# An attention kernel's PSUM banks: from a fixed rotation to a queue in which the sixth transposition bank behind a score piece is the first one's

## The chip, the cores and the metric

The kernel runs on one core of one Trainium2 chip, in float32 throughout. The time is the device time of one launch in microseconds (us); the kernel before has a median of 2784.84 us over three runs (2784.79 to 2785.24). A profile of one further execution shows what each engine did: TensorE (PE in the views, with its weight loads apart as PEld), VectorE (DVE), ScalarE (ACT), GpSimd (POOL) and SyncE (SP), which issues the DMAs.

## The reference, cut to what matters

An encoder layer over a short context (2 x 77 tokens) and a decoder layer over 2 x 2048 tokens, of width 512 with 16 heads of 32. The part that the change touches is the decoder's causal self-attention with a bias by relative distance:

```python
q, k, v = ...                                   # 16 heads of 32, each 2048 tokens, two batches
scores = jnp.einsum('bhqd,bhkd->bhqk', q, k) / jnp.sqrt(hd)
scores = scores + bias[None]                    # by distance; -inf above the diagonal
attn = jax.nn.softmax(scores, axis=-1)
out = jnp.einsum('bhqk,bhkd->bhqd', attn, v)
```

After it come the cross-attention to the 77 encoded tokens and a feed-forward of width 2048.

## The kernel before, in words

**Units.** The self-attention is cut into 128 units (b, m, g, t): batch b, block m of 512 queries (0 to 3), group g of four heads (0 to 3), tile t of 128 queries (0 to 3). A unit has n = 4m + t + 1 key tiles of 128 keys. `pieces` (L315) cuts them into pieces of up to four: n = 6 gives 4 + 2, n = 13 gives 4 + 4 + 3 + 2.

**Scores.** `scores` (L357) takes a piece: four banks of PSUM, one for each head of the group; one matmul for each head (L374; the four heads use four row groups of the array and run side by side). VectorE then empties the four banks in the order of the heads, with L383 for key tiles far from the diagonal and L390 for the last two, which get the bias; in a unit's last piece a head can need both. After the last piece comes the maximum of maxima (L399, tile `nm`), and four exponentials on ScalarE (L404) are put in a list, from which `exps` issues one or two at a time at fixed places.

**Turns.** `turn` (L410) transposes the probabilities of up to two pieces of a unit, so with m above 0 up to eight key tiles. For each key tile, called a load here, it takes one bank, makes four transpositions into it (L424, one for each head) and has the bank copied to SBUF: by ScalarE (L430) for the first half of the loads, by VectorE (L428) for the second. Behind the fourth load it issues one exponential, behind the last another. `values` (L435) then multiplies the copies with the value rows (L441) into bank 7.

**Order.** All engines take their instructions in program order. The loop at L1730 goes through the turns: the scores of a piece further on are issued as soon as their probabilities' place is free, which in nearly all cases is right ahead of a turn; then the turn; then, at a unit's end, a `slot` of other work (projections at L215 and L1018, normalisations at L305, cross-attention, all with banks of their own); more scores; an exponential or two; the values.

**Banks.** Of the eight banks of PSUM, bank 7 belongs to `values`. The other seven go round: `bank()` (L179) hands out 0, 1, ... 6, 0, ... to whoever asks. Scores take four in a row, a turn one for each load. An instruction that writes into a bank waits until the bank's last reader is done. After the attention, `count` is set so that only banks 0 to 3 go round, and the feed-forward uses 4 to 7 by an order of its own.

**Which bank is whose.** Call the seven banks just behind a score piece a, b, c (the oldest) and s0 to s3 (the piece's heads). With the rotation the loads of the turn that follows take a, b, c, s0, s1, s2, s3, a. The eighth load meets the first load's bank again, and loads four to seven write into the banks that VectorE empties of the scores.

Transpositions with m = 0 are cut in another way (`first`, four loads for each piece) and have no more than four loads in a turn.

Of the kernel before, what the change touches and what calls it, by code (L numbers as in the profile page):

```python
# [22 lines left out]
HC = P // HD  # L23
# [31 lines left out]
def tile_encoder_decoder(ctx: ExitStack, tc: tile.TileContext, ins, out):  # L55
# [103 lines left out]
    with (  # L159
# [14 lines left out]
        oT_all = ac.tile([P, 6, TB * P], F32, name="oT")  # L174
        bo = ac.tile([P, D], F32, name="row_dec_sa_out_b")
        psum = ps.tile([P, 8, 512], F32, name="psum")
        count = {"bank": 0, "banks": 7, "pts": 0, "oT": 0, "mm": 0}

        def bank():  # L179

            i = count["bank"] % count["banks"]
            count["bank"] += 1
            return psum[:, i, :]

        def in_turn(what, tile):
            i = count[what] % tile.shape[1]
            count[what] += 1
            return tile[:, i, :]

        def rows4(r):  # L190
            return slice(r * HD, (r + 1) * HD)
# [19 lines left out]
        def q_job(b, m, g):  # L211
            def run(w):
                mm = bank()
                for c in range(NC):
                    nc.tensor.matmul(mm, w[:, c, :], nTs[b, m][:, c, :], start=(c == 0), stop=(c == NC - 1))  # L215
                q = sb.tile([P, MB], F32, name="q", tag="q", bufs=3)
                nc.vector.tensor_scalar(q, mm, vec("dec_sa_in_b", g), SCALE, ALU.add, ALU.mult)
                qTs[b, m, g] = q

            return lambda: small_w(g * P), run, True  # L220

        def k_job(b, m, g):
            def run(w):
                mm = bank()
                for c in range(NC):
                    nc.tensor.matmul(mm, w[:, c, :], nTs[b, m][:, c, :], start=(c == 0), stop=(c == NC - 1))
                d, bi = kT[:, g, ts(m, MB)], vec("dec_sa_in_b", NC + g)
                if m >= 2:
                    nc.vector.tensor_scalar(d, mm, bi, None, ALU.add)
                else:  # L230
                    nc.scalar.activation(d, mm, AF.Identity, bias=bi)

            return lambda: small_w(D + g * P), run, True

        def v_job(b, m, t):
            def run(w):
                mm = bank()
                for c in range(NC):
                    nc.tensor.matmul(
                        mm, nTs[b, m][:, c, ts(t, P)], w[:, c, :], start=(c == 0), stop=(c == NC - 1)  # L240
                    )
                nc.vector.tensor_copy(vv[:, m * TB + t, :], mm)

            return lambda: big_w("v"), run, False
# [99 lines left out]
        def probabilities(n):  # L344
            w = (units[n][1] + 1) * MB
            at = END - HC * w if n % 2 else 0
            p = pp[:, at : at + HC * w].rearrange("p (k r x) -> p r k x", r=HC, x=P)
            return [p[:, r] for r in range(HC)]
# [3 lines left out]
        def exps(k):  # L352

            for _ in range(min(k, len(late_exps))):
                late_exps.pop(0)[1]()

        def scores(n, k0, kn):  # L357
            b, m, g, t = units[n]
            i = m * TB + t
            if k0 == 0:  # L360
                state[n] = {
                    "p": probabilities(n),
                    "mx": sm.tile([P, HC, 8], F32, name="mx", tag="mx"),
                    "nm": sm.tile([P, HC], F32, name="nm", tag="nm"),
                    "col": 0,
                }
                if t == 0:
                    sums_of[b, m, g] = sm.tile([P, TB, HC], F32, name="sums", tag="sums")
            st = state[n]
            last = k0 + kn == i + 1  # L370
            q = qTs[b, m, g]
            banks = [bank() for _ in range(HC)]
            for r in range(HC):
                nc.tensor.matmul(  # L374
                    banks[r][:, : kn * P], q[rows4(r), ts(t, P)], kT[rows4(r), g, k0 * P : (k0 + kn) * P],
                    start=True, stop=True,
                )
            far = max(0, kn - 2) if last else kn
            col = st["col"]
            for r in range(HC):  # L380
                p, s, c = st["p"][r], banks[r].rearrange("p (k x) -> p k x", x=P), col
                if far:
                    nc.vector.tensor_scalar(  # L383
                        p[:, k0 : k0 + far], s[:, :far], 1.0, None, ALU.mult, ALU.max,
                        accum_out=st["mx"][:, r, c : c + 1],
                    )
                    c += 1
                if last:
                    near = biases[b, m, g][:, r, :].rearrange("p (k x) -> p k x", x=P)
                    nc.vector.tensor_tensor_reduce(  # L390
                        p[:, k0 + far : i + 1], s[:, far:kn], near[:, 2 - (kn - far) :], 1.0, LOWEST, ALU.add, ALU.max,
                        accum_out=st["mx"][:, r, c : c + 1],
                    )
                    c += 1
            st["col"] = c
            if not last:
                return

            nc.vector.tensor_reduce(st["nm"], st["mx"][:, :, :c], AX.X, ALU.max, negate=True)  # L399
            for r in range(HC):  # L400
                p, nm, to = st["p"][r][:, : i + 1], st["nm"][:, r : r + 1], sums_of[b, m, g][:, t, r : r + 1]

                def run(p=p, nm=nm, to=to):
                    nc.scalar.activation(p, p, AF.Exp, bias=nm, accum_out=to)  # L404

                late_exps.append((n, run))
# [3 lines left out]
        def turn(pieces):  # L410

            first = units[pieces[0][0]][1] == 0
            loads = []
            for n, k0, kn in pieces:
                ks = range(k0, k0 + kn)
                if first:
                    loads += [[(n, k, r) for k in ks] for r in range(HC)]
                else:
                    loads += [[(n, k, r) for r in range(HC)] for k in ks]
            for o, load in enumerate(loads):  # L420
                pt = bank()
                pts = in_turn("pts", pts_all).rearrange("p (x q) -> p x q", q=P)
                for x, (n, k, r) in enumerate(load):
                    nc.tensor.transpose(pt[:, ts(x, P)], state[n]["p"][r][:, k], ident)  # L424
                    got[n, k, r] = pts[:, x, :]
                w = len(load) * P
                if o % 2 if first else o >= (len(loads) + 1) // 2:
                    nc.vector.tensor_copy(pts[:, : len(load), :], pt[:, :w])  # L428
                else:
                    nc.scalar.copy(pts[:, : len(load), :], pt[:, :w])  # L430
                if not first and o == min(3, len(loads) - 1):
                    exps(1)
            exps(HC if first else 1)
# [634 lines left out]
        for x, (b, m) in enumerate(blocks):  # L1068
            u = x * NU
            first = m == 0  # L1070
# [11 lines left out]
            else:  # L1082
# [8 lines left out]
                for at, names in todo.items():  # L1091
                    for name in names.split():
                        i = int(name[1])
# [140 lines left out]
        def late_loads():  # L1234
            nc.vector.tensor_scalar(qbias, vecs[:, _COL["dec_ca_in_b"] : _COL["dec_ca_in_b"] + NC], SCALE, None, ALU.mult)
            for t in range(TB):
                new_y(1, t)
            nc.sync.dma_start(kTc, ckT_d[:, :, :S])
            for _ in range(2):
                t = sb.tile([P, HC, 2 * P], F32, name="bias", tag="bias", bufs=2)  # L1240
                qT.append(t.rearrange("p (g a) k -> p g (a k)", g=2))
# [478 lines left out]
        def score_next():  # L1720
            n, k0, kn = stream[at[0]]
            scores(n, k0, kn)
            scored_to[n] = k0 + kn
            at[0] += 1
# [4 lines left out]
        i = 0  # L1729
# [28 lines left out]
        for t in (2, 3):  # L1758
            residual_load(*blocks[-1], t, pts_all[:, 2 * t - 3, :])
        late_loads()  # L1760
        count.update(bank=0, banks=4)
        side = cross(1)
        slot(end)
        for s in range(4):
# [58 lines left out]
```

## Time and profile before

| what | us |
|---|---|
| median of three runs | 2784.84 |
| lowest, highest | 2784.79, 2785.24 |
| the profiled execution's own time | 2785.57 |
| its span in the profile | 2783.8 |
| self-attention: last transposition starts at | 1706.9 |

The profile's page gives each engine's busy time over the span, and groups of instructions by line. The views used below are: the page; the timeline, which lists instructions of one engine in order of time and joins those that follow each other without idle time (start, duration, engine, line, operation, output <- inputs, shape, count, and in brackets the idle time before with what ended it); the waits, which sum idle time by line and by what ended it; and windows, which give busy time of every engine within stretches of the span. A row of weight loads (PEld) is the better witness for TensorE's progress here than a row of matmuls, since a matmul's row reaches over the next one's start: a weight load starts when its instruction may start. In timeline rows times are rounded to 0.01 us.

### The profile page before, as it was taken

What the parts mean: (1) busy time and instruction counts of PE and PEld (TensorE: products, weight loads), DVE (VectorE), ACT (ScalarE), POOL (GpSimd) and SP (SyncE); (2) the same over time, 40 slices, a digit from 0 to 9 for tenths busy, and PEclk for the clock granted to TensorE, in tenths of its full rate; (3) what the DMA queues carried; (4) which work ended last, traced back from release to release, by engine and by line L of the source; (5) the groups of instructions that cost most, each with busy time, mean ns of one, the idle gap of its engine ahead of it and who ended that gap; (6) DMA issues with size and microseconds to landing.
All of it is one profiled execution on the core that took longest, in us unless ns stands there. A gap on an engine that the chain in (4) does not pass through costs nothing. (4 is left out here: it accounts for less than half of the span.)

```text
span 2783.8 us, 66824 instructions
## 1 busy us (share of the span) xinstructions
PE 2757.1 (99%) x26294; PEld 2137.0 (77%) x26294; DVE 1885.9 (68%) x5412; ACT 1439.6 (52%) x2761; POOL 915.2 (33%) x777
## 2 busy tenths in 40 slices
PE   9999999999999999999999999999999999999998
PEld 5577776677666566676677667898989898989898
DVE  5676587788887578687788895555555646464645
ACT  3544455656666556666656665434444444444431
POOL 1501134400100412212300002364646474746456
PEclk9999999999999999999999999999999999999999
DMA  7423345421112521233211004574748575656475
GB/s 224 140 88 110 111 129 161 128 59 38 38 55 58 142 76 55 89 100 103 96 55 40 25 32 138 182 236 155 230 155 233 179 224 162 221 163 222 147 227 182
DMA packets 282252, 362.45 MB, mean 130 GB/s; under 512 B 39073, under 2 KB 156625, under 8 KB 281811
## 3 DMA queue, kind: packets, MB, share of 16 engines
q1 hardware_dynamic: 281938, 358.18, 42.0%
q8 instruction: 208, 3.41, 0.5%
q14 instruction: 106, 0.86, 0.1%
HBM read 314.49 MB, written 43.59 MB: 129 GB/s over the span
## 5 line engine op out<-in xcount | busy, mean ns | idle before, releaser
L404 ACT ACTIVATE pp<-pp,nm 128x128 f32<-128x128 f32 (+15 forms) x512 | 612.1, 1202 | 143.8 <-DVE nm L399 139.3
L383 DVE TENSOR_SCALAR_CACHE_REDUCE pp<-psum 128x512 f32<-128x512 f32 (+3 forms) x1024 | 558.9, 591 | 59.1 <-PE psum L374 57.4
L424 PEld LDWEIGHTS psum<-ident,pp 128*128 128x128 f32 x4352 | 475.8, 142 | 110.0 <-DVE pp L383 56.0
L430 ACT COPY pts<-psum 128x512 f32<-128x512 f32 (+3 forms) x592 | 300.9, 576 | 474.1 <-PE psum L424 342.8
L424 PE MATMUL psum<-ident,pp 128*128 128x128 f32 x4352 | 538.3, 278 | 7.6 <-ACT nT L310 2.3
L428 DVE COPY pts<-psum 128x512 f32<-128x512 f32 (+2 forms) x544 | 330.1, 660 | 65.8 <-PE psum L424 65.1
L374 PE MATMUL psum<-kT,q 32*128 32x512 f32 (+3 forms) x2560 | 358.7, 574 | 3.8 <-DVE pp L383 1.9
L441 PEld LDWEIGHTS psum<-pts,vv 128*32 128x32 f32 x8704 | 225.8, 110 | 126.0 <-issue 115.6
L1523 PE MATMUL psum<-pp 128*128 128x128 f32 x2560 | 304.5, 276 | 1.9 <-POOL pp L936 1.6
L1523 PEld LDWEIGHTS psum<-pp 128*128 128x128 f32 x2560 | 296.3, 192 | 8.6 <-issue 2.8
L441 PE MATMUL psum<-pts,vv 128*32 128x128 f32 x8704 | 279.5, 275 | 2.4 <-DVE pts L428 1.7
L936 POOL TENSOR_TENSOR pp<-pp 128x512 f32<-128x512 f32 x159 | 212.7, 1354 | 128.1 <-DMA pp<-in_dec_ff_wT_dram 68.9
L1494 PE MATMUL psum<-vv,pp 128*128 128x256 f32 x1024 | 236.2, 381 | 0.0
L374 PEld LDWEIGHTS psum<-kT,q 32*128 32x128 f32 x2560 | 122.8, 183 | 122.8 <-issue 79.6
L1494 PEld LDWEIGHTS psum<-vv,pp 128*128 128x128 f32 x1024 | 190.5, 190 | 25.6 <-issue 0.5
L390 DVE CUSTOM_DVE_ANT_0 pp<-psum,bias 128x256 f32<-128x256 f32 (+1 forms) x512 | 196.1, 411 | 15.7 <-PE psum L374 15.6
L1507 DVE TENSOR_TENSOR kT<-kT,psum 128x512 f32<-128x512 f32 x96 | 65.8, 686 | 190.7 <-PE psum L1494 190.6
L1494 PE MATMUL psum<-nT,pp 128*128 128x256 f32 x768 | 174.1, 380 | 0.0
L1510 ACT ACTIVATE kT<-kT,vecs 128x256 f32<-128x256 f32 x192 | 87.0, 501 | 156.7 <-DVE kT L1507 156.0
L1494 PEld LDWEIGHTS psum<-nT,pp 128*128 128x128 f32 x768 | 144.3, 190 | 20.2 <-issue 1.6
L469 POOL TENSOR_TENSOR oT<-rirows,oT 128x512 f32<-128x512 f32 x30 | 38.3, 1275 | 368.9 <-DMA rirows<-rec 214.2
L1531 ACT COPY oT<-psum 128x128 f32<-128x128 f32 x56 | 14.9, 267 | 239.2 <-PE psum L1523 239.2
(242 smaller groups left out, 3908.5 us busy)
## 6 DMA issues: line engine op xcount, KB each, us to landing
pp<-w_d SPq DMA_DIRECT2D x520, 256.0 KB
pp<-in_dec_ff_wT_dram SPq DMA_DIRECT2D x112, 256.0 KB
wqk<-in_dec_sa_in_wT_dram SPq DMA_DIRECT2D x76, 256.0 KB
bias<-tzg SPq DMA_DIRECT2D x128, 128.0 KB
pp<-wo_d SPq DMA_DIRECT2D x56, 256.0 KB
vv<-in_enc_ff_wT_dram SPq DMA_DIRECT2D x8, 1024.0 KB
xr<-in_x_dram SPq DMA_DIRECT2D x32, 256.0 KB
vv<-y SPq DMA_DIRECT2D x32, 256.0 KB
```

What stands on the lines that cost most here:

```text
L374: nc.tensor.matmul(banks[r][:, : kn * P], q[rows4(r), ts(t, P)], kT[rows4(r), g, k0 * P : (k0 + kn) * P], start=True, stop=True,)
L383: nc.vector.tensor_scalar(p[:, k0 : k0 + far], s[:, :far], 1.0, None, ALU.mult, ALU.max, accum_out=st["mx"][:, r, c : c + 1],)
L390: nc.vector.tensor_tensor_reduce(p[:, k0 + far : i + 1], s[:, far:kn], near[:, 2 - (kn - far) :], 1.0, LOWEST, ALU.add, ALU.max, accum_out ...
L404: nc.scalar.activation(p, p, AF.Exp, bias=nm, accum_out=to)
L424: nc.tensor.transpose(pt[:, ts(x, P)], state[n]["p"][r][:, k], ident)
L428: nc.vector.tensor_copy(pts[:, : len(load), :], pt[:, :w])
L430: nc.scalar.copy(pts[:, : len(load), :], pt[:, :w])
L441: nc.tensor.matmul(ot[rows4(r), t, :], vv[:, k, ts(g * HC + r, HD)], got.pop((n, k, r)), start=(k == 0), stop=(k == i),)
L936: engine.tensor_tensor(out, a, b, ALU.subtract)
L1494: nc.tensor.matmul(mm[:, ts(f, TOK)], a[:, c, ts(f, P)], b[:, c, :], start=fresh and f == 0 and c == 0, stop=c == 1, skip_group_check=True,)
L1510: nc.scalar.activation(dst[:, e, :], src[:, e, :], AF.Relu, bias=vec("dec_ff1_b", f + e))
L1523: nc.tensor.matmul(psum[:, bank_i, ts(col, P)], lhs[:, c, :], w[:, c, :], start=fresh and k in (0, 3) and c == 0, stop=c == 3, skip_group_ ...
```

## The change

The counter of the rotation becomes a list, `ring`, of the seven banks in order of last use. `bank()` takes the list's head and puts it at the end, which by itself is the same rotation. `scores` remembers its four banks in `scored`. A turn looks whether these four are the last four used (no other work took a bank in between); if so, and if it is not a turn of m = 0, its sixth load (o == 5) takes the list's third entry instead of the head. Behind a score piece the list is then s2, s3, a, b, c, s0, s1, so that the third entry is a, the first load's bank. The loads then take a, b, c, s0, s1, a, s2, s3.

```diff
-        count = {"bank": 0, "banks": 7, "pts": 0, "oT": 0, "mm": 0}
+        count = {"pts": 0, "oT": 0, "mm": 0}
+        ring, scored = list(range(7)), []
 
         def bank():
 
-            i = count["bank"] % count["banks"]
-            count["bank"] += 1
-            return psum[:, i, :]
+            return psum[:, take(ring[0]), :]
+
+        def take(i):
+            ring.remove(i)
+            ring.append(i)
+            return i
...
             banks = [bank() for _ in range(HC)]
+            scored[:] = ring[-HC:]
...
+            behind_scores = ring[-HC:] == scored
             for o, load in enumerate(loads):
-                pt = bank()
+                if o == 5 and behind_scores and not first:
+                    pt = psum[:, take(ring[2]), :]
+                else:
+                    pt = bank()
...
-        count.update(bank=0, banks=4)
+        ring[:] = range(4)
```

No instruction is added, removed or moved in any engine's order; what changes is which bank some transpositions, and the users of banks after them, write into, and with it whom they wait for.

## The prediction

> **What bounds the kernel now.** I read the page first, then the waits of TensorE's weight loads, then windows over the blocks of queries, then the timeline turn by turn.
>
> ```profile
> PE 2757.1 (99%) x26294; PEld 2137.0 (77%) x26294; DVE 1885.9 (68%) x5412; ACT 1439.6 (52%) x2761; POOL 915.2 (33%) x777
> L424 PEld LDWEIGHTS psum<-ident,pp 128*128 128x128 f32 x4352 | 475.8, 142 | 110.0 <-DVE pp L383 56.0
> L383 DVE TENSOR_SCALAR_CACHE_REDUCE pp<-psum 128x512 f32<-128x512 f32 (+3 forms) x1024 | 558.9, 591 | 59.1 <-PE psum L374 57.4
> L430 ACT COPY pts<-psum 128x512 f32<-128x512 f32 (+3 forms) x592 | 300.9, 576 | 474.1 <-PE psum L424 342.8
> PEld psum L424 <- DVE pp L383: 56.0, 93, 0.8
> PEld psum L424 <- DVE mx L390: 8.6, 33, 0.5
> 620.00:868.00 248.00, 247.60 (x3094) 173.58 (x3093) 215.33 (x684) 167.75 (x240) 20.57 (x16) 1.00 0.14 41
> ```
>
> TensorE is the bound: 99% busy. VectorE is not far behind in places: 215.33 of 248 us in the block m = 3 (the number ahead of x684). Most of the 56.0 us before L424 is no loss: it is the ordinary pause between the last score matmul's weight load and the first transposition, while the scores still run. The 8.6 us behind L390 are closer to the matter: transpositions inside a turn that wait until VectorE has emptied a head's bank. The measure of a turn without waits is this (block m = 2, t = 3):
>
> ```profile
> 426.35 3.48 PEld L424 LDWEIGHTS psum<-ident,pp 128*128 128x128 f32 x32 [0.20 <-issue]
> 441.68 3.04 PEld L424 LDWEIGHTS psum<-ident,pp 128*128 128x128 f32 x28 [0.20 <-issue]
> ```
>
> 32 transpositions in 3.48 us, the last of them 0.14 long (page): 0.108 each, so 0.44 for a load of four, while VectorE needs 0.59 on average (page, L383) for a head's far tiles alone. TensorE can outrun VectorE from the fourth load on.
>
> **The change part by part.** No instruction is added, removed or moved, so only waits count. By the new order loads six, seven and eight take a, s2, s3 instead of s2, s3, a: the heads' banks are needed one load, 0.44 us, later, and the sixth load waits for ScalarE's copy of the first load. What follows the turn gets banks of the same age or older: after eight loads the next four (b, c, s0, s1) are unchanged; after seven the first is s3 instead of a, after six s2 and s3 instead of s3 and a. I went through all 107 turns of six or more loads that stand behind a score piece (112 by the code, 16 of six loads, 24 of seven, 72 of eight; five have other work or a turn ahead of them). Each kind occurs once per batch and head group, so eight times.
>
> *Six loads (m = 1, t = 1).*
>
> ```profile
> 183.05 0.97 PEld L424 LDWEIGHTS psum<-ident,pp 128*128 128x128 f32 x8
> 184.16 0.30 PEld L215 LDWEIGHTS psum<-nT,wqk 128*128 128x128 f32 x2
> 183.47 0.09 DVE L390 DVE_READ_ACCUMULATOR2_ANT mx<- 128x1 f32 x1
> 184.02 0.09 DVE L390 DVE_READ_ACCUMULATOR2_ANT mx<- 128x1 f32 x1
> ```
>
> The sixth load waited for the third head (done 183.56), the job after it for the fourth (done 184.11, started 184.16: the release takes 0.05). Now the sixth load follows without a wait at about 183.44 and the job, on the third head's bank, at 183.87: 0.29 earlier. In the other seven, where fewer loads waited ahead, I count 0.24: 8 x 0.24 = 1.9 us.
>
> *Seven loads (m = 1, t = 2).*
>
> ```profile
> 195.58 2.72 PEld L424 LDWEIGHTS psum<-ident,pp 128*128 128x128 f32 x24 [0.76 <-issue]
> 198.57 0.42 PEld L424 LDWEIGHTS psum<-ident,pp 128*128 128x128 f32 x4 [0.27 <-DVE mx L390]
> 198.96 1.60 PEld L1018 LDWEIGHTS psum<-wqk,xt 128*128 128x128 f32 x8
> 198.43 0.08 DVE L390 DVE_READ_ACCUMULATOR2_ANT mx<- 128x1 f32 x1
> 196.28 2.05 ACT L430 COPY pts<-psum 128x512 f32<-128x512 f32 x4 [7.66 <-PE psum L424]
> ```
>
> ScalarE's first copy is done near 196.8, long before the sixth load. Without waits the seven loads would end at 195.58 + 28 x 0.108 = 198.60, and the job at L1018, now on the fourth head's bank (198.51 + 0.05), can start there: 0.36 earlier. Seven of the eight turns wait so: 2.5 us.
>
> *Eight loads (m = 3, t = 1 and t = 2).*
>
> ```profile
> 638.05 3.67 PEld L424 LDWEIGHTS psum<-ident,pp 128*128 128x128 f32 x32 [0.55 <-DVE pp L383]
> 655.81 2.71 PEld L424 LDWEIGHTS psum<-ident,pp 128*128 128x128 f32 x24 [0.76 <-DVE pp L383]
> 658.79 0.86 PEld L424 LDWEIGHTS psum<-ident,pp 128*128 128x128 f32 x8 [0.27 <-DVE mx L390]
> 659.82 0.31 PEld L374 LDWEIGHTS psum<-kT,q 32*128 32x128 f32 x8 [0.17 <-issue]
> 658.87 2.47 DVE L428 COPY pts<-psum 128x512 f32<-128x512 f32 x4
> ```
>
> The first loses 3.67 - 3.48 = 0.19, all of which goes: 8 x 0.19, one of them less, 1.4 us. The second lasts 655.81 to 659.65, 0.36 too long, but the scores behind it need the fifth load's bank, whose copy is the first of four VectorE copies: 658.87 + 0.68, and 0.05 for the release, 659.60 against 659.82. So 0.22, not 0.36; seven turns, in one of which values follow and the cap is absent: 1.7 us.
>
> *The second turns of m = 3 (six, seven, eight loads).*
>
> ```profile
> 645.91 2.60 PEld L424 LDWEIGHTS psum<-ident,pp 128*128 128x128 f32 x24 [0.76 <-DVE pp L383]
> 648.59 0.30 PEld L215 LDWEIGHTS psum<-nT,wqk 128*128 128x128 f32 x2
> 663.84 3.10 PEld L424 LDWEIGHTS psum<-ident,pp 128*128 128x128 f32 x28 [0.76 <-DVE pp L383]
> 646.00 0.69 DVE L383 TENSOR_SCALAR_CACHE_REDUCE pp<-psum 128x512 f32<-128x512 f32 x1 [0.15 <-PE psum L374]
> ```
>
> 3.10 against 3.04: 0.05 in some 13 turns. In four with six loads the job waits for the fourth head's bank (648.59; the loads end at 645.91 + 24 x 0.108 = 648.50) and would not: 0.1 each. Together 1.1 us. The last row is what lets gains of the turn ahead pass: VectorE had been waiting 0.15 for these scores, so it moves up with them.
>
> *Where the new wait costs.* In m = 2 the tiles t = 3 and t = 0 have an exponential ahead of ScalarE's first copy, twelve turns of sixteen:
>
> ```profile
> 427.35 1.26 ACT L404 ACTIVATE pp<-pp,nm 128x1152 f32<-128x1152 f32 x1 [3.97 <-DVE nm L399]
> 428.61 2.02 ACT L430 COPY pts<-psum 128x512 f32<-128x512 f32 x4
> 430.00 0.49 PEld L374 LDWEIGHTS psum<-kT,q 32*128 32x128 f32 x4 [0.17 <-issue]
> 430.68 0.30 PEld L374 LDWEIGHTS psum<-kT,q 32*128 32x128 f32 x4 [0.20 <-ACT pts L430]
> 431.74 0.37 PEld L441 LDWEIGHTS psum<-pts,vv 128*32 128x32 f32 x15 [0.76 <-issue]
> 434.78 0.69 DVE L383 TENSOR_SCALAR_CACHE_REDUCE pp<-psum 128x512 f32<-128x512 f32 x1 [1.06 <-PE psum L374]
> 445.93 0.29 PEld L374 LDWEIGHTS psum<-kT,q 32*128 32x128 f32 x2 [0.20 <-ACT pts L430]
> ```
>
> The first copy ends at 428.61 + 0.58 = 429.19 (0.58 is a copy's mean on the page), so the sixth load, at 426.35 + 20 x 0.108 = 428.5 now, starts at 429.24: 0.7 late. But the scores behind the turn already wait for ScalarE: their last heads start at 430.68, because the fourth copy ends at 430.63. A turn 0.7 later ends where those heads start, so nothing is lost. In t = 0 (0.66 late by the same count) the last head starts at 445.93 in the same way. Cover gone, it would be 12 x 0.7 = 8.4 us. VectorE's copies of the last three loads come 0.7 later too; what is late next would be the eviction of those scores, and VectorE has 1.06 to spare before the piece that follows (434.78). I take 0, bounds 0 and 8.4.
>
> One turn has no cover, at the end of the first batch (exponentials of 1.99 ahead):
>
> ```profile
> 867.52 3.04 PEld L424 LDWEIGHTS psum<-ident,pp 128*128 128x128 f32 x28 [0.20 <-issue]
> 870.95 0.30 PEld L215 LDWEIGHTS psum<-nT,wqk 128*128 128x128 f32 x2 [0.39 <-ACT pts L430]
> 868.35 1.99 ACT L404 ACTIVATE pp<-pp,nm 128x2048 f32<-128x2048 f32 x1
> 870.34 2.01 ACT L430 COPY pts<-psum 128x512 f32<-128x512 f32 x4
> ```
>
> The sixth load now stands at 870.95, where the job stood, and the job behind two loads at 871.77: 0.8 lost.
>
> Here a rule speaks against the change. The Trainium skill ("Perfetto Trace Analysis", section "Matmuls") wants independent matmul groups to rotate through different banks, so that one's evacuation overlaps the next one's matmuls; a load that returns to a bank five loads old gives up overlap. The rows of m = 2 agree that it costs a wait; the rows of m = 1 and m = 3 disagree, since there the oldest bank is not the one that is free first. By the rule alone the sum would be the waits of m = 2 and this last one, some 9 us the other way.
>
> **The sum.** 1.9 + 2.5 + 1.4 + 1.7 + 1.1 = 8.6, less 0.8: 7.8 us. Whether it reaches the end:
>
> ```profile
> 1707.00:2784.00 1077.00, 1068.59 (x8278) 966.81 (x8276) 584.85 (x1125) 427.39 (x912) 594.49 (x504) 1.00 0.62 193
> ```
>
> None of the sixty longest waits of the weight loads is ended by a DMA, and behind the attention TensorE is busy for all but 8 us, so an earlier attention ends the kernel earlier. The sum is made in an execution of 2785.57 us (span 2783.8, 1.8 around it), 0.73 above the median; 7.8 less is 2777.8 there and **2777.0** on the median's scale.
>
> **The rivals.**
>
> *VectorE keeps m = 3's gains.* It is 87% busy there; earlier scores would only queue. For: the 0.22 cap. Against: the 0.15 idle. Without the 4.2 us of m = 3: 2784.84 - 4.4 + 0.8 = 2781.2.
>
> *The waits of m = 2 are not covered.* For: the sixth load does stand 0.7 late. Against: 430.68 and 445.93. 2777.0 + 8.4 = 2785.4.
>
> *The slower side: ScalarE's late copy spreads.* In m = 2 the sixth load's wait is uncovered, and by delaying three VectorE copies it puts the next evictions back, so that the next turn's fourth and fifth loads wait as well, a load's 0.44 more. 12 x 1.14 + 0.8 - 8.6 = +5.9: 2790.7. It decides if the scores behind such a turn end later than now. This is also what the Trainium skill's rule above ("Perfetto Trace Analysis", "Matmuls") would bring about. Against it stand the heads that wait at 430.68.
>
> *The change does nothing*, since other work takes banks between scores and turns: 2784.8. Against: 107 of 112 turns.
>
> **How the numbers follow.** The forecast 0.73, VectorE's rival 0.13, uncovered 0.06, spread 0.05, nothing 0.03. The forecast's own range: with half of m = 1's gains absorbed 2779.2; with the cap lifted (0.14 x 8), the 0.8 absorbed and the small class twice as large 2774.0. The range reaches to VectorE's rival and a little over: 2774.0 to 2782.5; it leaves out the last three rivals and the forecast's edges. A change of 0.2%, 5.6 us, is about what a measurement can tell; faster needs less than 2779.3. That is the forecast but for its edge: 0.72. Slower is the spread: 0.05; the rest, 0.23, within.
>
> **What would show it.** Right: in m = 1, t = 2 one row of 28 transpositions of about 3.0 us and the job 0.36 earlier; in m = 3, t = 1 32 in 3.48. In m = 2, t = 3 an idle time of 0.7 before twelve transpositions, ended by ACT L430, and the eight score loads behind it in one row with the values at the same distance from the turn's start as now (5.39). After 1707 us no difference but the shift. Wrong: a longer distance there, or idle time before L374 in m = 3, ended by L428, that eats the gains.

## The result, and the profile after

| | before | changed |
|---|---|---|
| median, us (15 runs each) | 2784.77 | 2778.48 |
| lowest, highest | 2782.03, 2787.39 | 2777.06, 2783.56 |
| the profiled execution's own time | 2785.57 | 2777.06 |
| its span | 2783.8 | 2775.2 |

The ratio is 0.998, with an interval of 0.9973 to 0.9986: 3.9 to 7.5 us less. The forecast was 2777.0 in a range of 2774.0 to 2782.5.

The lines of the code move by a few: L424 is now L433, L374 is L379, L383 is L388, L390 is L395, L404 is L409, L428 is L437, L430 is L439, L441 is L450, L215 is L219 and L1018 is L1027. The page first, then the waits of the weight loads (line, what ended the wait, sum in us, how often, longest).

```profile
span 2775.2 us, 66804 instructions
PE 2743.2 (99%) x26294; PEld 2132.2 (77%) x26294; DVE 1886.3 (68%) x5412; ACT 1439.0 (52%) x2761; POOL 915.1 (33%) x777
L433 PEld LDWEIGHTS psum<-ident,pp 128*128 128x128 f32 x4352 | 474.6, 141 | 109.7 <-DVE pp L388 60.6
```

```profile
PEld psum L433 <- DVE mx L395: 2.3, 10, 0.5
PEld psum L433 <- ACT pts L439: 11.0, 15, 1.5
```

The same view of the kernel before, behind ScalarE's copies:

```profile
PEld psum L424 <- ACT pts L430: 1.3, 2, 0.8
```

All counts of instructions are the same. The page hardly shows where the time went: the idle time before the transpositions is 109.7 us after 110.0. The waits do. Behind VectorE's last read of a head's bank 23 waits have gone, from 8.6 us in 33 to 2.3 in 10. Behind ScalarE's copies 9.7 us have come: 15 waits of 11.0 together, where the kernel before has two of 1.3. New waits are longer than the removed ones, and yet the kernel is faster. A forecast that sums the waits has the wrong sign.

The removed waits, in the timeline of the weight loads (start, duration; the turns that the prediction shows at 195.58, 638.05 and 655.81):

```profile
194.62 3.04 PEld L433 LDWEIGHTS psum<-ident,pp 128*128 128x128 f32 x28 [0.76 <-issue]
197.62 1.60 PEld L1027 LDWEIGHTS psum<-wqk,xt 128*128 128x128 f32 x8
...
634.85 3.48 PEld L433 LDWEIGHTS psum<-ident,pp 128*128 128x128 f32 x32 [0.55 <-DVE pp L388]
...
652.31 3.48 PEld L433 LDWEIGHTS psum<-ident,pp 128*128 128x128 f32 x32 [0.76 <-DVE pp L388]
655.96 0.44 PEld L379 LDWEIGHTS psum<-kT,q 32*128 32x128 f32 x8 [0.17 <-issue]
```

Each turn is now one row at the pace without waits, 3.04 for seven loads and 3.48 for eight. In m = 1, t = 2 the job starts 3.00 behind the turn's start instead of 3.38. In m = 3, t = 2 the scores start 3.65 behind it instead of 4.01, but their row takes 0.44 where a row of eight without a wait takes 0.31 (the row at 428.88 below): some of its heads wait for VectorE's copy of the fifth load. So 0.36 of the loads becomes 0.23 in time. That is the cap of the prediction.

The new waits, in m = 2 (t = 3 at 424.56) and in the one turn at the end of the first batch (862.01), and what ScalarE does there:

```profile
424.56 2.17 PEld L433 LDWEIGHTS psum<-ident,pp 128*128 128x128 f32 x20 [0.20 <-issue]
427.42 1.29 PEld L433 LDWEIGHTS psum<-ident,pp 128*128 128x128 f32 x12 [0.70 <-ACT pts L439]
428.88 0.31 PEld L379 LDWEIGHTS psum<-kT,q 32*128 32x128 f32 x8 [0.17 <-ACT pts L439]
429.95 1.69 PEld L450 LDWEIGHTS psum<-pts,vv 128*32 128x32 f32 x64 [0.76 <-issue]
...
862.01 2.16 PEld L433 LDWEIGHTS psum<-ident,pp 128*128 128x128 f32 x20 [0.20 <-issue]
865.68 0.86 PEld L433 LDWEIGHTS psum<-ident,pp 128*128 128x128 f32 x8 [1.51 <-ACT pts L439]
866.50 0.30 PEld L219 LDWEIGHTS psum<-nT,wqk 128*128 128x128 f32 x2
```

```profile
426.81 2.03 ACT L439 COPY pts<-psum 128x512 f32<-128x512 f32 x4
...
863.08 1.99 ACT L409 ACTIVATE pp<-pp,nm 128x2048 f32<-128x2048 f32 x1
865.07 2.01 ACT L439 COPY pts<-psum 128x512 f32<-128x512 f32 x4
```

The first 20 transpositions (five loads) follow each other, and the sixth load waits 0.70 us for the first of four copies, which starts at 426.81. The eight score loads behind, which came in two rows of four 0.68 apart, now come in one. From the turn's start to the values it is 429.95 - 424.56 = 5.39 us, to the hundredth as before (431.74 - 426.35). In the late turn there is no such second wait: from its start to the job behind it it is 4.49 instead of 3.43.

To see every turn, I compared the starts of the 26,294 weight loads, which stand in the same order in both traces. The table gives the median over the turns of a kind of what the time from a turn's first weight load to the next turn's became less (us; a minus is a longer turn; e1 to e7 are the experiments below):

```
kind of turn (how many)       change   e1    e2    e3    e4    e5    e6    e7
m=1 t=1, six loads (8)          0.24  0.24  0.00  0.00  0.24  0.00  0.23  0.23
m=1 t=2, seven (8)              0.37  0.37  0.00  0.00  0.37  0.00  0.37  0.37
m=2 t=0, seven (8)              0.00  0.00  0.00  0.00 -0.02  0.96  0.41  0.96
m=2 t=3, eight (8)             -0.01  0.00 -0.01  0.00 -0.45  0.69 -0.01  0.69
m=3 t=1, eight (8)              0.19  0.00  0.00  0.19  0.19  0.00  0.19  0.19
m=3 t=1, second turn, six (8)   0.05  0.00  0.00  0.05  0.05  0.00  0.05  0.05
m=3 t=2, eight (8)              0.24  0.00  0.00  0.24  0.24  0.00  0.24  0.24
m=3 t=2, second turn, seven (7) 0.06  0.00  0.00  0.06 -0.17  0.00  0.06  0.06
the one late turn (1)          -1.07  0.00 -0.01 -1.07 -1.50 -0.01 -1.07  0.00
```

Added up over the turns themselves (not the medians), but without what a dip of TensorE's clock moved in five of them (last section), the change gains 1.45 + 2.7 in m = 1 and 1.47 + 1.79 + 0.9 in m = 3, and loses 0.1 in m = 2 and 1.07 in the late turn: 7.1 us. Behind 1707 us nothing more is added.

### The profile page after: what moved, and what is told of

It is laid out like the page before. It is cut to its first block, busy times and chain, and to the rows that moved or that the text cites. A ratio compares the mean times of both kernels' runs of the same rounds, so it can differ in the third digit from the quotient of the medians.

```text
span 2775.2 us, 66804 instructions
## 1 busy us (share of the span) xinstructions
PE 2743.2 (99%) x26294; PEld 2132.2 (77%) x26294; DVE 1886.3 (68%) x5412; ACT 1439.0 (52%) x2761; POOL 915.1 (33%) x777
## 5 line engine op out<-in xcount | busy, mean ns | idle before, releaser
L409 ACT ACTIVATE pp<-pp,nm 128x128 f32<-128x128 f32 (+15 forms) x512 | 612.1, 1203 | 143.2 <-DVE nm L404 139.0
L388 DVE TENSOR_SCALAR_CACHE_REDUCE pp<-psum 128x512 f32<-128x512 f32 (+3 forms) x1024 | 558.7, 591 | 55.6 <-PE psum L379 53.5
L433 PEld LDWEIGHTS psum<-ident,pp 128*128 128x128 f32 x4352 | 474.6, 141 | 109.7 <-DVE pp L388 60.6
L433 PE MATMUL psum<-ident,pp 128*128 128x128 f32 x4352 | 530.8, 277 | 13.1 <-ACT pts L439 7.1
L439 ACT COPY pts<-psum 128x512 f32<-128x512 f32 (+3 forms) x592 | 300.6, 576 | 467.9 <-PE psum L433 337.9
L437 DVE COPY pts<-psum 128x512 f32<-128x512 f32 (+2 forms) x544 | 331.2, 660 | 67.3 <-PE psum L433 66.7
L379 PE MATMUL psum<-kT,q 32*128 32x512 f32 (+3 forms) x2560 | 351.9, 575 | 4.5 <-DVE pp L388 1.9
L450 PEld LDWEIGHTS psum<-pts,vv 128*32 128x32 f32 x8704 | 226.6, 110 | 126.5 <-issue 115.5
L450 PE MATMUL psum<-pts,vv 128*32 128x128 f32 x8704 | 280.9, 276 | 2.6 <-DVE pts L437 1.8
L379 PEld LDWEIGHTS psum<-kT,q 32*128 32x128 f32 x2560 | 118.2, 183 | 121.0 <-issue 78.4
L395 DVE CUSTOM_DVE_ANT_0 pp<-psum,bias 128x256 f32<-128x256 f32 (+1 forms) x512 | 196.4, 412 | 15.3 <-PE psum L379 15.3
```

The lines of the kernel that those rows point to most:

```text
L379: nc.tensor.matmul(banks[r][:, : kn * P], q[rows4(r), ts(t, P)], kT[rows4(r), g, k0 * P : (k0 + kn) * P], start=True, stop=True,)
L388: nc.vector.tensor_scalar(p[:, k0 : k0 + far], s[:, :far], 1.0, None, ALU.mult, ALU.max, accum_out=st["mx"][:, r, c : c + 1],)
L395: nc.vector.tensor_tensor_reduce(p[:, k0 + far : i + 1], s[:, far:kn], near[:, 2 - (kn - far) :], 1.0, LOWEST, ALU.add, ALU.max, accum_out ...
L450: nc.tensor.matmul(ot[rows4(r), t, :], vv[:, k, ts(g * HC + r, HD)], got.pop((n, k, r)), start=(k == 0), stop=(k == i),)
```

## The experiments

Theory: the kernel gains where the sixth load waited for VectorE, in m = 1 and in m = 3 apart from each other, and the new wait of m = 2 is paid for by a wait that stood behind it already. Rivals: m = 3 gives nothing because VectorE is the bound there; m = 2 costs what its waits add up to; m = 1's gain is taken back later.

**One block at a time (e1, e2, e3).** Three kernels exchange the bank in the turns of one block only.

```diff
-                if o == 5 and behind_scores and not first:
+                if o == 5 and behind_scores and units[pieces[0][0]][1] == 1:
```

The others have `== 2` and `== 3` there.

> The sixth bank is exchanged in the turns of m = 1 only. My theory (the heads' banks are needed a load later, and only turns in which a head's bank was late gain): each of the eight turns of six loads 0.24 us shorter, each of seven turns of seven loads 0.37, nothing elsewhere: 4.5 us less than before, about 2780.3 us. Rival (the gain comes from m = 3, where VectorE is busiest): under 1 us.

> The sixth bank is exchanged in the turns of m = 2 only. My theory (the wait for ScalarE's first copy is covered by the scores behind the turn, which wait for ScalarE's later copies anyway): an idle time of 0.7 us before twelve transpositions in 12 turns, and yet the same time as before, within 0.3 us but for the clock. Rival (the wait is paid): 8.4 us more, about 2793.

> The sixth bank is exchanged in the turns of m = 3 only. My theory: 0.19 in eight turns, 0.22 to 0.44 in seven, 0.05 to 0.1 in seventeen, less 0.8 to 1.1 in the one late turn at the end of the first batch: 3.2 us less than before, about 2781.6. Rival (VectorE, 87% busy there, keeps the gains): 0.8 us more than before.

| | median, us | ratio to before (2785.23 in these runs) | interval |
|---|---|---|---|
| m = 1 alone | 2780.97 | 0.9987 | 0.9978 to 0.9996 |
| m = 2 alone | 2784.80 | 1.0001 | 0.9991 to 1.001 |
| m = 3 alone | 2781.34 | 0.9987 | 0.9978 to 0.9997 |

m = 2 alone decides between the theory and a sum of waits. Its waits, and its timeline at t = 3:

```profile
PEld psum L433 <- ACT pts L439: 9.8, 14, 1.0
PEld psum L433 <- DVE mx L395: 8.5, 33, 0.5
```

```profile
425.15 2.17 PEld L433 LDWEIGHTS psum<-ident,pp 128*128 128x128 f32 x20 [0.20 <-issue]
428.02 1.29 PEld L433 LDWEIGHTS psum<-ident,pp 128*128 128x128 f32 x12 [0.70 <-ACT pts L439]
429.48 0.31 PEld L379 LDWEIGHTS psum<-kT,q 32*128 32x128 f32 x8 [0.17 <-ACT pts L439]
430.55 1.69 PEld L450 LDWEIGHTS psum<-pts,vv 128*32 128x32 f32 x64 [0.76 <-issue]
```

Twelve waits are added, 9.8 - 1.3 = 8.5 us, nothing is taken away, and the time stands still: 0.43 us less by the medians, with an interval of 2.5 less to 2.8 more, which leaves out the 8.4 of the rival. Again 5.40 from the turn's start to the values. (In this execution one of the twelve turns, at 557.2 us, is 0.35 longer: VectorE's work ahead of ScalarE's exponential came that much later there. The same turn loses nothing in the changed kernel.) m = 1 alone and m = 3 alone each gain, 4.3 and 3.9 us by the medians, so VectorE doesn't keep m = 3's gain. The table shows their rows at the same values alone as together: turn by turn the parts add. The medians are too coarse for that: 4.3, 3.9 and 0.4 make 8.6, where the change as a whole gave 6.3, and each of these numbers has an interval of some 2 us or more to either side.

**The fifth load in place of the sixth (e4).** If the exchange is a matter of who frees a bank first, an earlier exchange should gain the same in m = 1 and m = 3, and lose in m = 2 as soon as the wait is longer than its cover.

```diff
-                if o == 5 and behind_scores and not first:
-                    pt = psum[:, take(ring[2]), :]
+                if o == 4 and behind_scores and not first:
+                    pt = psum[:, take(ring[3]), :]
```

> The exchange is made one load earlier: the fifth load takes the first load's bank, the heads' banks follow from the sixth on. My theory: in m = 2 the wait for ScalarE's first copy now starts 0.44 us earlier and reaches over its cover: the six turns of t = 3 cost 0.44 each (2.6 us), those of t = 0 nothing, since their scores wait for a fourth copy that comes late enough; the one late turn costs 0.44 more; the gains of m = 1 and m = 3 stay as with the sixth. 4.9 us less than before instead of 7.9: about 2780. Rival (a wait for ScalarE is hidden in m = 2 whatever its length): as the change, 2777 to 2778.5. Rival (an earlier exchange helps the heads more): faster than the change.

2780.84 us, ratio 0.9989 (0.9979 to 0.9999). The change's own ratio, 0.998, lies at the edge of this interval, so the time alone hardly decides against the rival of a wait that is always hidden; the turns do. The timeline at m = 2, t = 3:

```profile
423.48 1.73 PEld L433 LDWEIGHTS psum<-ident,pp 128*128 128x128 f32 x16 [0.20 <-issue]
426.35 1.73 PEld L433 LDWEIGHTS psum<-ident,pp 128*128 128x128 f32 x16 [1.14 <-ACT pts L439]
428.25 0.31 PEld L379 LDWEIGHTS psum<-kT,q 32*128 32x128 f32 x8 [0.17 <-issue]
429.32 1.69 PEld L450 LDWEIGHTS psum<-pts,vv 128*32 128x32 f32 x64 [0.76 <-issue]
```

The wait is now 1.14, 0.44 longer (one load), and the values come 5.84 behind the turn's start: 0.45 is lost, just what the wait exceeds its cover by. This is so in six of the eight turns of t = 3; in t = 0 the longer wait costs 0.02. So the cover does not hide a wait of whatever length: in t = 3 it is 0.7 us wide, and the sixth load's wait fills it to the brim. The gains of m = 1 and m = 3 are the same as with the sixth load, with two exceptions. The second turns with seven loads lose 0.17 instead of gaining 0.06. And the edit also reaches the sixteen turns of five loads, which the expectation left out: their fifth load now takes the first load's bank. Two of them gain 0.39, two 0.07 and 0.10, the others nothing, together 1.0 us.

**Take the cover away (e5, e6).** What covers the wait is that the scores need the banks of ScalarE's four copies, which stand behind an exponential. If VectorE copies two of these four (it has 1.06 us to spare there), the scores should come earlier by themselves, in the order of banks of before; and in the changed kernel the exchange should then cost its wait, which was free so far.

```diff
+                by_vector = len(loads) > 6 and units[pieces[0][0]][1] == 2 and units[pieces[0][0]][3] in (0, 3)
-                if o % 2 if first else o >= (len(loads) + 1) // 2:
+                if o % 2 if first else o >= (2 if by_vector else (len(loads) + 1) // 2):
```

First in the kernel before (e5):

> The bank order of before; in the twelve or so turns of m = 2 with t = 0 or 3 and more than six loads (sixteen in all) VectorE copies the third and fourth load instead of ScalarE. This takes away the wait of the scores behind these turns. My theory: these scores start 0.68 us earlier for t = 3 and 0.97 for t = 0, six turns each, so 9.9 us less than before, about 2775; bounds 6 and 10. Rival (VectorE, 80% busy in m = 2, pays it back with later evictions): the same as before.

2776.20 us against 2784.90 (ratio 0.9967, 0.9956 to 0.9979), 8.7 us less without any change of banks. The timeline of the weight loads and of ScalarE at m = 2, t = 3:

```profile
427.40 3.48 PEld L424 LDWEIGHTS psum<-ident,pp 128*128 128x128 f32 x32 [0.20 <-issue]
431.04 0.31 PEld L374 LDWEIGHTS psum<-kT,q 32*128 32x128 f32 x8 [0.17 <-issue]
432.11 0.92 PEld L442 LDWEIGHTS psum<-pts,vv 128*32 128x32 f32 x36 [0.76 <-issue]
```

```profile
428.39 1.26 ACT L404 ACTIVATE pp<-pp,nm 128x1152 f32<-128x1152 f32 x1 [3.69 <-DVE nm L399]
...
429.65 1.05 ACT L431 COPY pts<-psum 128x512 f32<-128x512 f32 x2
```

ScalarE's copies end at 430.70, before the turn does, and the values come 4.71 behind the turn's start instead of 5.39. Turn by turn, six of t = 0 gain 0.96 and six of t = 3 gain 0.67 to 0.71; the two of t = 3 with g = 3 gain nothing, and the two of t = 0 with g = 0, which have no exponential ahead of the copies, lose 0.42 each. That makes 9.1.

Then the same edit in the changed kernel (e6):

> The changed kernel, and the copies of m = 2 as in the run e5_copies. My theory: with the cover of the sixth load's wait gone, the wait for ScalarE's first copy is paid in m = 2: 0.68 in six turns and about 0.6 in six, 7.7 us more than the two parts add up to: 9.9 + 7.9 - 7.7 = 10 us less than before, about 2774.7. Rival (the wait was hidden by something else than those scores): 17.8 us less, about 2767.

2776.63 us, ratio 0.9972 (0.9963 to 0.9981). The two don't add: the change alone gives 6.3, the copies alone 8.7, both together 8.3. The timeline at the same place:

```profile
424.60 2.17 PEld L433 LDWEIGHTS psum<-ident,pp 128*128 128x128 f32 x20 [0.20 <-issue]
427.46 1.29 PEld L433 LDWEIGHTS psum<-ident,pp 128*128 128x128 f32 x12 [0.70 <-ACT pts L440]
428.92 0.31 PEld L379 LDWEIGHTS psum<-kT,q 32*128 32x128 f32 x8 [0.17 <-issue]
430.00 1.69 PEld L451 LDWEIGHTS psum<-pts,vv 128*32 128x32 f32 x64 [0.76 <-issue]
```

The scores no longer wait for ScalarE, but the sixth load does, and the values are back at 5.40. In t = 0 the copies still gain 0.41 of their 0.96 (table).

**Both, without the exchange where ScalarE is late (e7).**

```diff
+            late = units[pieces[0][0]][1] == 2 or units[pieces[0][0]] == (0, NMB - 1, NC - 1, 2)
-                if o == 5 and behind_scores and not first:
+                if o == 5 and behind_scores and not first and not late:
```

> The sixth bank is exchanged in m = 1 and m = 3 only, and not in the one late turn (first batch, m = 3, last head group, t = 2); the copies of m = 2 as in e5_copies. My theory: 9.9 from the copies, 4.5 from m = 1, 4.2 from m = 3: 18.6 us less than before, about 2766.2, and 12.3 less than the changed kernel. Rival (e5's gain does not exist or is bound to the bank order of before): about 2776.

2765.30 us against 2784.90, ratio 0.993 (0.9918 to 0.9943): the fastest of all these kernels, 13 us below the changed one. Page and timeline:

```profile
span 2763.1 us, 66815 instructions
```

```profile
423.99 3.48 PEld L434 LDWEIGHTS psum<-ident,pp 128*128 128x128 f32 x32 [0.20 <-issue]
427.63 0.31 PEld L379 LDWEIGHTS psum<-kT,q 32*128 32x128 f32 x8 [0.17 <-issue]
428.70 1.69 PEld L452 LDWEIGHTS psum<-pts,vv 128*32 128x32 f32 x64 [0.76 <-issue]
...
856.70 3.04 PEld L434 LDWEIGHTS psum<-ident,pp 128*128 128x128 f32 x28 [0.20 <-issue]
860.14 0.30 PEld L219 LDWEIGHTS psum<-nT,wqk 128*128 128x128 f32 x2 [0.40 <-ACT pts L441]
```

The values are at 4.71 again, and the late turn is as long as before the change (3.44 from its start to the job). The condition of the edit names a unit, so the turn ahead of the late one is left out of the exchange too.

Between this kernel and the one ahead of it lie 11.3 us. Six turns of t = 0 give 0.55 each and six of t = 3 give 0.70: 7.5 in m = 2. With its cover gone, the exchange costs close to the 8.4 that the prediction put on it as an upper bound. The late turn gives back 1.07, and the turn ahead of it no longer gains its 0.24, which makes 8.3. By the two profiles the other 3.0 go with TensorE's clock (last section): in that of the kernel ahead the granted clock is 0.91 over 460 to 480 us and 0.91 over 1290 to 1310, here it is 1.00 in both, and one turn at each place is 1.5 us shorter. The kernel before has 0.91 in both places as well, so the 19.6 us by the medians are not all due to banks and copies. Added up over the turns without these two, the profile shows 17.1 us, where 18.6 were expected.

## Why the prediction was right, point by point

*The sign and the size.* The forecast of 2777.0 was 1.5 us below the median. By the turns the banks gave 7.1 us where the sum had 7.8, which is just outside the interval of 3.9 to 7.5. No term is off by more than 0.45, and the misses go both ways, so that a part of the agreement is luck. The profiles' spans differ by 8.6, and most of what is left of that goes with the clock (last section).

*Six loads, m = 1, t = 1: 1.9 predicted, 1.45 found.* Six turns gave 0.24 as counted. The two of head group g = 1 gave nothing: the scores behind them wait for VectorE's copies, which stand behind the statistics of a normalisation, and that wait grew by as much as the turn became shorter. The statistics (L282) and the three copies behind them, on VectorE in the kernel before:

```profile
244.29 0.68 DVE L282 BATCH_NORM_STATS2 bnst<-xt 128x6 f32<-128x512 f32 x1
245.30 1.88 DVE L428 COPY pts<-psum 128x512 f32<-128x512 f32 x3
```

The wait of these scores, in the kernel before and in the last experiment:

```profile
246.03 0.29 PEld L374 LDWEIGHTS psum<-kT,q 32*128 32x128 f32 x2 [0.76 <-DVE pts L428]
```

```profile
244.94 0.29 PEld L379 LDWEIGHTS psum<-kT,q 32*128 32x128 f32 x2 [1.01 <-DVE pts L439]
```

0.76 became 1.01. The prediction counted what the turn loses and did not look, in each of the eight, for what stands behind it.

*Seven loads, m = 1, t = 2: 2.5 and 2.7.* 0.37 in a turn for 0.36. m = 1 alone gained 4.3 us by the medians, for 4.4 predicted in the two terms.

*Eight loads, m = 3: 1.4 + 1.7 and 1.47 + 1.79.* The cap by VectorE's copy is real: 0.23 to 0.24 in time out of 0.36 in the loads. *Second turns: 1.1 and 0.9.*

*m = 2: 0 predicted, 0.1 found*, with 8.2 us of new waits (11.0 less the 1.3 of before and the late turn's 1.51). This was the step on which the sign hung. It was right for the reason given, as m = 2 alone shows from one side and the removed cover from the other. Here the rule of the Trainium skill ("Perfetto Trace Analysis", section "Matmuls") can be weighed once more: independent groups should rotate through different banks. The last two kernels agree with it where the bank that comes back is ScalarE's late one (7.5 us), and m = 1 and m = 3 alone disagree where it is free earlier than the oldest (4.3 and 3.9 us gained). What decides in these runs is when a bank's reader is done, and rotation is only one guess at that.

*The late turn: 0.8 predicted, 1.07 found.* The prediction put the sixth load at 870.95, the job's old place, and the job two loads later, 0.82. The other 0.24 are the gain of the turn ahead of it, m = 3, t = 2 like the others. TensorE came earlier by that much, ScalarE did not: its first copy starts 2.82 behind the turn's start before (870.34 - 867.52) and 3.06 after (865.07 - 862.01). So the wait grew by the gain. The last experiment exchanges in neither turn, and there the two change by nothing.

*The rivals.* VectorE as the keeper of m = 3's gain fell with m = 3 alone; the uncovered and the spreading wait with m = 2 alone; no effect with the result's interval.

## What to carry to other kernels

A wait that is added costs only what it exceeds the next wait behind it by, so look for the instruction that waits last for the same engine, and measure the distance from the start of the group to that one: in m = 2, t = 3, 0.7 us of wait were free, and the next 0.44 were paid in full. The bank to take next is the one whose reader finishes first, which depends on what stands ahead of the reader in its own engine's queue; an exchange that gains where ScalarE's copy is early adds a wait where the copy stands behind an exponential. A wait that covers another is itself worth removing: in sixteen turns two copies given to the other engine were worth more than the banks (8.7 us against 6.3), but in the changed kernel only once the exchange was taken back there.

## What was not expected of the hardware

The clock granted to TensorE drops to half for 3.4 us at a time, or for two or three times as long. Windows over the kernel before (range, length, busy time of PE, PEld, DVE, ACT and POOL, granted clock, share and rate of DMA):

```profile
466.00:469.30 3.30, 2.56 (x24) 0.91 (x21) 3.23 (x13) 3.30 (x5) 0.83 (x2) 1.00 0.00 0
469.30:472.70 3.40, 3.40 (x20) 3.36 (x17) 2.50 (x15) 2.21 (x5) 3.05 (x2) 0.50 0.02 5
472.70:476.00 3.30, 3.30 (x38) 2.37 (x40) 2.60 (x5) 3.08 (x5) 0.00 (x0) 0.99 0.00 0
```

and over the changed one:

```profile
240.00:255.00 15.00, 14.82 (x135) 10.70 (x132) 13.64 (x63) 9.17 (x18) 4.17 (x4) 0.89 0.33 111
460.00:480.00 20.00, 19.26 (x184) 11.97 (x176) 18.20 (x64) 17.26 (x27) 5.42 (x5) 1.00 0.09 27
```

The turn that starts in the dip shows what it costs: its transpositions start 0.213 us apart at 0.50, and 0.109 behind it. The dip follows 3.3 us in which TensorE ran only 24 matmuls, waiting for the scores to be emptied. Ahead of its last microseconds the trace of the kernel before has four such stretches and the changed one's five, at other places: at 469 us before and none there after, at 246.7 after and none there before. The last experiment's has one, at 116 us. In single turns they moved a profile by up to 1.6 us, as much as lies between 7.1 and 8.6, and so two spans alone can't tell a change of this size to a microsecond. The Trainium skill ("TensorE: Matmul & The Clock Gate", section "What's actually happening") gives a free-running window of 3413 ns and half clock after an idle one; the length and the half agree with these rows, but TensorE was not idle, only thinly used, for by the profile 2.56 of the 3.30 us ahead are busy.

A wait for a bank costs a little less than it lasts. After one, the second weight load of a turn follows in 0.057 to 0.060 us in most cases instead of 0.109, so about 0.05 is made up at once: the row of 12 behind the wait at 427.42 lasts 1.29 us, where 12 at the pace without waits would take 1.33.
